# Cross-attention with layer norm: the last two tiles' probabilities transposed on TensorE, and a new order for the last ten tiles

## The chip, the cores and the metric

One NeuronCore of a Trainium2 chip. The metric is the device time of one execution in microseconds; the time before is the median of three runs.

## The reference

`x` has 4 batches of 2048 rows of 512, the context 4 batches of 77 rows of 512; there are 16 heads of 32, and everything is f32.

```python
qs = (q @ wq).reshape(Bq, Lq, H, HD).transpose(0, 2, 1, 3)
ks_ = (k @ wk).reshape(Bq, Lk, H, HD).transpose(0, 2, 1, 3)
vs = (v @ wv).reshape(Bq, Lk, H, HD).transpose(0, 2, 1, 3)
scores = jnp.einsum('bhqd,bhkd->bhqk', qs, ks_) / jnp.sqrt(jnp.float32(HD))
scores = jnp.where(mask[:, None, :, :], -jnp.inf, scores)
attn_w = jax.nn.softmax(scores, axis=-1)
attn = jnp.einsum('bhqk,bhkd->bhqd', attn_w, vs)
attn = attn.transpose(0, 2, 1, 3).reshape(Bq, Lq, H * HD)
out = attn @ wo + q
mu = jnp.mean(out, axis=-1, keepdims=True)
var = jnp.mean((out - mu) ** 2, axis=-1, keepdims=True)
return (out - mu) / jnp.sqrt(var + EPS) * gamma + beta
```

The queries `q` are `x`; keys and values both come from the context, and the mask says which of the 77 keys a batch leaves out.

## The kernel before

The 8192 rows are worked through in 64 tiles of 128 rows (tile 0 to 63); two tiles make a block, four a group, 16 a batch. The keys and values of all batches are made once at the start and stay in SBUF. To keep f32 accuracy at the speed of TensorE's rounded f32 type (`F32R`), the large products take three matmuls: both operands are split into a rounded high part and the remainder, and high×high, high×low and low×high are added in PSUM.

A tile goes through these steps. The letter is the one that names the step in the written order.

- `Q`, `q` (`q_visit`, `q_evac`): a quarter of a group's queries on TensorE (12 matmuls), copied from PSUM by VectorE. `i`, `j` split the transposed input `xT` into `xth` and `xtl` on ScalarE and GpSimd.
- `S` (`scores`): the scores of the 16 heads in four PSUM banks, plain f32, small matmuls packed into parts of the array.
- `T` (`maxima`, four quarters per tile) on VectorE: adds the mask and finds each head's maximum, into `pbuf`. `e` (`exps`, four quarters) on ScalarE: exponential and sum.
- `r` and `n` on VectorE and GpSimd: reciprocal of the sums, and the probabilities times it. `h` and `m` are the same for half of the heads.
- `t` (`transp`) on VectorE: transposes `pbuf` in 32×32 squares into `B`. `P` (`regroup_part`): 12 DMAs per block, from SBUF to SBUF, gather the squares into `PT`, where the keys lie along the partitions, 96 of them (77, and 19 again, so that even and odd heads can share one layout). For the last block each tile has 12 DMAs of its own, `U` (`regroup_tile`).
- `V` (`av`, per block) or `W` (`av_tile`, per tile): probabilities times values on TensorE. `a`, `b` split the result into `AH` on ScalarE and `AL` on VectorE; `c` and `d` do it for one tile.
- `O` (`o_proj`): the output projection, 12 matmuls of 512 columns. `+` (`residual`): VectorE adds the row of `x` that `x` (`load_x`) loaded. For four tiles `X` (`resid`) adds it in PSUM instead, as a plain f32 matmul with the identity.
- The layer norm, on whichever engine the order names: `s` statistics on VectorE, or `I` and `J` mean and squares on ScalarE; `u` the reciprocal root on GpSimd; then `y` (centre, times gamma) and `z` (times the root, plus beta) on VectorE, or `k` (ScalarE) or `p` (GpSimd) with `f` (gamma and beta on GpSimd), or `K` (times the root, on ScalarE) and `G` (plus beta, on GpSimd). `M` copies gamma or beta into a PSUM bank. `w` stores on SyncE's queue.

Tiles 0 to 53 run in a loop with a fixed order. For the last ten tiles the order is a written list, `ORDER`: words like `T63.2` (step, tile, part) or `P30.4g` (with the engine whose queue issues the DMA: `s`, `a`, `g`). Every engine carries out its own instructions in the order in which the words stand, and waits in it where data or a buffer is missing. PSUM's eight banks are given out in turn by `bank()`, except those that `M` has taken.

Of the kernel before, what the change touches and what calls it, by code (L numbers as in the profile page):

```python
# [8 lines left out]
F32 = mybir.dt.float32  # L9
# [8 lines left out]
P = 128  # L18
# [20 lines left out]
CUT = 27  # L39

# [5 lines left out]
i31 S54 Q59 T54.2 e54.2 x50 k46 T54.1 j31 T54.0 x56 q58 T54.3 S55 x59 O49 q59 e54.1 e54.3 T55.1 T55.0 T55.2 t53  # L46
e54.0 e55.1 S56 r54 P26.7g Q61 x61 x58 k47 T55.3 e55.3 V25 P26.2s T56.3 n54 x51 T56.0 e55.0 +49 x57 P26.3s e55.2 f46
P26.4s T56.1 T56.2 q61 S57 a25.0 t54 r55 n55 T57.0 e56.1 P26.9s T57.1 b25.0 s49 P26.1g w46 Q63 T57.2 P26.0s O48
a25.1 b25.1 S58 e56.0 t55 e56.3 P27.8s e56.2 Q62 T57.3 q63 P26.6g e57.2 Q60 P26.10g e57.0 f47 r56 P26.8s e57.1 T58.2
P26.11s T58.3 T58.1 T58.0 P26.5g P27.1s x52 x60 +48 P27.7g e57.3 P27.3s e58.3 n56 P27.0g e58.1 S59 P27.10g q62 t56  # L50
r57 s48 V26 q60 e58.2 T59.0 a26.1 T59.1 S60 e58.0 P27.2g T59.2 P27.11g O51 n57 t57 e59.2 T59.3 P27.5g a26.0 e59.3
O50 T60.1 x53 P27.9s T60.3 r58 T60.0 +51 b26.1 e59.0 b26.0 P27.4s e59.1 T60.2 P27.6s e60.0 P28.6s P28.2g S61 P28.10s
u48 e60.2 P28.3s n58 t58 P28.1s +50 r59 T61.2 V27 T61.1 x54 P28.11s P28.7s T61.0 T61.3 O53 P28.4s e60.3 P28.8g n59
t59 w47 S62 P28.0g a27.1 b27.1 O52 P29.6g e60.1 a27.0 T62.2 s51 b27.0 e61.0 e61.3 P28.5s e61.1 P29.8g P28.9s T62.1
P29.2g r60 n60 O54 +53 T62.0 s50 S63 e61.2 T62.3 t60 e62.1 e62.3 P29.0g +52 u50 u51 x55 r61 T63.2 e62.0 O55 n61
T63.0 P29.3s e62.2 +55 T63.1 P29.9s P29.7s t61 V28 +54 P29.4s P29.10s P29.5s T63.3 p50 a28.0 b28.0 a28.1 P29.11s M0
r62 P29.1s x62 P30.3s e63.3 f50 s55 P30.2s P30.1s V29 P30.10s P30.7g n62 b28.1 y55 P30.9s a29.0 v51 a29.1 P30.5s X59
P30.6s b29.0 P30.4s s54 O56 I52 P30.11s P30.8s t62 e63.0 e63.1 y48 e63.2 P30.0g U62.7s u54 b29.1 k51 u55 h63.0 w50
O57 m63.0 +56 h63.1 I56 U62.9s U62.3s O59 U62.11s U62.6s U62.0g s53 y52 U62.8s U62.2s V30 m63.1 J52 M1 x63 a30.0 s59
t63 y59 U62.5a +57 U62.4a U63.9a J56 O58 y49 U63.3s U63.8s U63.10s z55 U62.1g b30.0 u49 a30.1 f51 X62 U63.2a U63.5s  # L60
b30.1 X61 U63.6s O60 u56 U63.1a y54 U63.0s z48 O61 w55 u53 U63.11s u52 z49 z54 U63.4a I57 y53 +58 U62.10a u59 p56
J57 I61 W62 z53 U63.7s f56 w51 +60 s58 u57 W63 z52 w48 u58 s60 z59 u60 X63 y60 w49 c62 w56 J61 y57 d62 w52 c63 d63
w59 w54 w53 z60 u61 O62 z57 w60 O63 p58 f58 y61 I62 z61 J62 w57 y62 u62 w58 s63 z62 w61 y63 u63 z63 w62 w63
# [4 lines left out]
def xattn_layernorm(  # L68
# [53 lines left out]
    ident = ident[:, :P]  # L122
    mhalf, mneg, gates = small[:, 0:2], small[:, 2:4], small[:, 4:5]
    pbuf = [const.tile([P, NP, PW], F32, name=f"pbuf{i}") for i in range(NPB)]
# [18 lines left out]

    def keys_of(h):
        return slice(TAIL_K, NK2) if h % 2 == 0 else slice(0, NK)
# [3 lines left out]
    od, pos, mvs, rns, vd, ris, ends = {}, {}, {}, {}, {}, {}, {}  # L149
# [160 lines left out]
    def maxima(t, lo, hi):  # L310
        pb = pbuf[t % NPB]
        mb = bat[t // TPB][0]
        nm = nmax[t]
        for h in HEADS[lo:hi]:
            g, j = divmod(h, GH)
            nc.vector.tensor_tensor_reduce(  # L316
                pb[:, h // 2, (h % 2) * NK : (h % 2 + 1) * NK],
                scs[t][j][:, g * NK : (g + 1) * NK],
                mb[:, t % TPB, keys_of(h)],
                -1.0,  # L320
                3.0e38,
                ALU.add,
                ALU.min,
                accum_out=nm[:, h : h + 1],
            )
# [22 lines left out]
    def half_view(ap, r):  # L348
        return ap.rearrange("p (g r a) -> p g r a", r=2, a=2)[:, :, r]
# [6 lines left out]
    def normalise_half(t, r):  # L356
        pv = pbuf[t % NPB].rearrange("p (g r) w -> p g r w", r=2)[:, :, r, : 2 * NK]
        pv = pv.rearrange("p g (a k) -> p g a k", a=2)
        rv = half_view(ris[t], r)[:, :, :, None]
        nc.gpsimd.tensor_tensor(pv, pv, rv.to_broadcast((P, NG, 2, NK)), ALU.mult)  # L360

    def transp(t):
# [3 lines left out]
        if b < NBLK - 1:  # L366
            bt = bts[b].rearrange("p c (q t r) -> p c q t r", q=NP, t=2)[:, :, :, tt, :]
        else:
            bt = bts[b].rearrange("p c (t q r) -> p c q t r", q=NP, t=2)[:, :, :, tt, :]
# [5 lines left out]
    def regroup_part(b, n, queue, cols=slice(0, 2 * NP * 32)):  # L375
# [12 lines left out]
    def regroup_tile(t, n, queue):  # L388
        tt = t % 2
        regroup_part(t // 2, n, queue, slice(tt * NP * 32, (tt + 1) * NP * 32))  # L390


    def av(b):
# [3 lines left out]
        for g in range(NG):  # L397
            for j in range(GH):
# [4 lines left out]
                    pt[:NK2, :, h % 2, h // 2].rearrange("p i t r -> p t i r"),  # L403
# [4 lines left out]
    def av_tile(t):  # L408
        b, tt = divmod(t, 2)
        pt = pts[b].rearrange("p i a (t q r) -> p i a t q r", q=NP, t=2)  # L410
        pas[b, tt] = bank(f"pa_{b}_{tt}")
        for g in range(NG):
            for j in range(GH):
# [3 lines left out]
                    vsb[:, t // TPB, HD * h : HD * (h + 1)],  # L417
                    pt[:NK2, :, h % 2, tt, h // 2],
# [19 lines left out]
    def load_x(t):  # L438
# [6 lines left out]
        else:  # L445
            if t // 2 not in ends:
                ends[t // 2] = sb.tile([P, 2, GRP], F32, tag="xtf", name=f"o_end_{t}")
            od[t] = ends[t // 2][:, t % 2]
        nc.sync.dma_start(od[t], x[t * P : (t + 1) * P, :])

    def resid(t):
        pos[t] = bank(f"po_{t}")
        nc.tensor.matmul(pos[t], ident, od[t], start=True, stop=False)

    def o_proj(t):
# [9 lines left out]
        for n, (_, c, a, w) in enumerate(prods):  # L465
            nc.tensor.matmul(pos[t], a[:, c, rs], w[:, c, :], start=(first and n == 0), stop=(n == 11))  # L466
# [36 lines left out]
    def moments_one(t):  # L503
        st = sb.tile([P, 6], F32, tag="st", bufs=3, name=f"st_{t}")
        nc.vector.bn_stats(st, pos.get(t, od[t]))
        mvs[t, 1] = sb.tile([P, 4], F32, tag="mvt", bufs=64 - LATE, name=f"mvt_{t}")
        nc.vector.bn_aggr(mvs[t, 1][:, :2], st)

    def act_mean(t):
        if "junk" not in ends:  # L510
            ends["junk"] = sb.tile([P, NG, GRP], F32, tag="q", name="junk")
        mvs[t, 1] = sb.tile([P, 4], F32, tag="mvt", bufs=64 - LATE, name=f"mvt_{t}")
        nc.scalar.activation(
            ends["junk"][:, t % NG], pos.get(t, od[t]), AF.Identity, scale=1.0 / D, accum_out=mvs[t, 1][:, 0:1]
        )

    def act_squares(t):
        mv = mvs[t, 1]
        nc.scalar.activation(
            ends["junk"][:, t % NG], pos.get(t, od[t]), AF.Square, bias=mv[:, 0:1], scale=-1.0, accum_out=mv[:, 1:2]  # L520
# [32 lines left out]
    def centre(t):  # L553
        row = gam if t in pos else rows.get(0, gam)
        nc.vector.scalar_tensor_tensor(od[t], pos.pop(t, od[t]), mvs[t, 1][:, 0:1], row, ALU.subtract, ALU.mult)

# [295 lines left out]
```

## Time and profile before

| | us |
|---|---|
| median of three runs | 515.69 (515.43 to 515.73) |
| profiled execution, its own time | 516.79 |
| span of the profiled execution, first to last instruction | 515.0 |
| TensorE (PE) busy | 503.8 |
| VectorE (DVE) busy | 473.5 |
| ScalarE (ACT) busy | 470.3 |
| GpSimd (POOL) busy | 418.7 |

All terms below are made against the span of 515.0 us. A row of the timeline gives the start, the duration, the engine, the line of the kernel, the operation, what it writes and reads, the shapes and a count; in brackets stands the idle time of the engine before it and what ended that. A matmul's duration reaches into the next one's, so the cost of a run of matmuls is the distance between starts. SPq, ACTq and the like are the queues that issue DMAs.

### The profile page before, as it was taken

Reading aid. Unit: us, or ns where it says so; the run is one execution under the profiler, and the core shown is the slowest. Engines: PE = TensorE matmul, PEld = TensorE weight load, DVE = VectorE, ACT = ScalarE, POOL = GpSimd, SP = SyncE. Lnnn points to the kernel's source line nnn. Section 1 sums busy time; section 2 is a strip of 40 time slices with the busy share of each in tenths; the row PEclk is TensorE's granted clock in tenths of the full one; section 3 lists DMA queues with packets and bytes.
Section 4 is the critical chain, followed back from the end, with each engine's and each line's share of the span. In section 5 each row is a group of like instructions: output and inputs, shape, how many; then the busy total and the mean of one; then the engine's idle time right before and its main releaser. Section 6 shows DMA issues by size and latency. Waiting matters only on the chain.

```text
span 515.0 us, 20430 instructions
## 1 busy us (share of the span) xinstructions
PE 503.8 (98%) x6836; PEld 385.2 (75%) x6836; DVE 473.5 (92%) x2572; ACT 470.3 (91%) x2240; POOL 418.7 (81%) x376
## 2 busy tenths in 40 slices
PE   8999999999999999999999999999999999999994
PEld 6987777777877777787777777777777777777672
DVE  6798999899998888999999899889999989899996
ACT  6798999999899999999899999999899999999841
POOL 1659349988898988888889989889889988857996
PEclk9999999999999999999999999999999999999999
DMA  8946876878887878787878888777868778786665
GB/s 319 396 138 162 208 187 178 227 200 206 228 214 208 231 211 229 215 205 202 212 206 224 234 218 214 203 198 223 227 193 229 200 207 233 183 222 176 175 210 209
DMA packets 58937, 110.24 MB, mean 214 GB/s; under 512 B 9393, under 2 KB 11313, under 8 KB 58833
## 3 DMA queue, kind: packets, MB, share of 16 engines
q1 hardware_dynamic: 56000, 103.36, 73.3%
q0 software_dynamic: 2128, 4.85, 3.5%
q8 instruction: 55, 0.90, 0.8%
q10 hardware_dynamic: 704, 0.72, 0.5%
q14 instruction: 50, 0.40, 0.2%
HBM read 41.79 MB, written 16.78 MB: 114 GB/s over the span
## 4 chain that ended last, share of the span: by engine, by line
PE 83%; DMA 5%; POOL 4%; DVE 4%; SPq 2%; issue 1%; ACT 0%; DVEq 0%; POOLq 0%
PE pq L170 30%; PE po L466 29%; PE sc L302 10%; PE pa L400 10%; DMA PT<-B 4%; SPq L382 2%; PE pv L236 2%; DVE B L370 1%; PE pk L196 1%; PE pq L599 1%; POOL mvt L532 1%; DVE pbuf L316 1%; POOL o_end L545 1%; DMA xtf<-xT 1%; POOL o_end L496 1%
## 5 line engine op out<-in xcount | busy, mean ns | idle before, releaser
L330 ACT ACTIVATE pbuf<-pbuf,nm 128x77 f32<-128x77 f32 x1024 | 352.5, 352 | 16.2 <-DVE nm L316 14.8
L330 ACT ACTIVATION_READ_ACCUMULATOR pbuf<-pbuf,nm 128x1 f32 x1024 | 196.9, 192 | 0.0
L316 DVE CUSTOM_DVE_ANT_0 pbuf<-sc,mb 128x77 f32<-128x77 f32 x1024 | 170.7, 230 | 23.3 <-PE sc L302 23.2
L346 POOL TENSOR_TENSOR pbuf<-pbuf,ri 128x1232 f32<-128x1232 f32 x63 | 142.2, 2258 | 22.9 <-DVE ri L341 16.1
L170 PE MATMUL pq<-xth,wqh 128*128 128x512 f32 (+1 forms) x256 | 98.8, 386 | 0.0
L170 PE MATMUL pq<-xtl,wqh 128*128 128x512 f32 (+1 forms) x256 | 97.9, 382 | 0.0
L170 PE MATMUL pq<-xth,wql 128*128 128x512 f32 (+1 forms) x256 | 97.9, 382 | 0.0
L370 DVE STREAM_TRANSPOSE B<-pbuf 128x1280 f32<-128x1280 f32 x64 | 95.5, 1493 | 2.2 <-DMA PT<-B 1.8
L466 PE MATMUL po<-woh,AH 128*128 128x512 f32 x232 | 96.9, 418 | 0.0
L466 PE MATMUL po<-wol,AH 128*128 128x512 f32 x232 | 90.6, 391 | 0.0
L466 PE MATMUL po<-woh,AL 128*128 128x512 f32 x232 | 88.9, 391 | 0.0
L316 DVE DVE_READ_ACCUMULATOR2_ANT nm<- 128x1 f32 x1024 | 84.0, 82 | 0.0
L496 POOL TENSOR_TENSOR o<-o,gam 128x512 f32<-128x512 f32 x50 | 65.6, 1311 | 14.1 <-ACT o L492 14.0
L302 PEld LDWEIGHTS sc<-kct,q 32*64 32x64 f32 x4096 | 51.6, 130 | 24.4 <-issue 23.0
L497 POOL TENSOR_TENSOR o<-o,bet 128x512 f32<-128x512 f32 x50 | 64.5, 1289 | 3.9
L163 POOL TENSOR_TENSOR xtl<-xtf,xth 128x1024 fp32r<-128x1024 f32 x28 | 67.1, 2397 | 0.0
L302 PE MATMUL sc<-kct,q 32*64 32x77 f32 x4096 | 62.1, 237 | 0.7 <-DVE nm L316 0.3
L400 PE MATMUL pa<-PT,vsb 96*32 96x256 f32 x960 | 58.0, 382 | 1.5 <-DMA PT<-B 1.2
L170 PEld LDWEIGHTS pq<-xth,wqh 128*128 128x128 f32 x256 | 48.1, 188 | 9.8
L170 PEld LDWEIGHTS pq<-xth,wql 128*128 128x128 f32 x256 | 48.1, 188 | 9.4
L170 PEld LDWEIGHTS pq<-xtl,wqh 128*128 128x128 f32 x256 | 48.1, 188 | 9.1
L466 PEld LDWEIGHTS po<-woh,AH 128*128 128x128 f32 x232 | 43.5, 187 | 13.0 <-issue 0.7
(141 smaller groups left out, 689.4 us busy)
## 6 DMA issues: line engine op xcount, KB each, us to landing
PT<-B SPq DMA_DIRECT2D x352, 128.0 KB, 2.9
xtf<-xT SPq DMA_DIRECT2D x28, 512.0 KB, 5.3
o<-x SPq DMA_DIRECT2D x56, 256.0 KB, 5.6
out<-o SPq DMA_DIRECT2D x56, 256.0 KB, 2.6
PT<-B POOLq DMA_DIRECT2D x20, 128.0 KB, 4.0
o_end<-x SPq DMA_DIRECT2D x8, 256.0 KB
out<-o_end SPq DMA_DIRECT2D x8, 256.0 KB, 2.1
xtf<-xT SPq DMA_DIRECT2D x4, 256.0 KB
```

The source lines that it names most:

```text
L163: nc.gpsimd.tensor_tensor(l, fx.pop((g, c)), h.bitcast(F32), ALU.subtract)
L170: nc.tensor.matmul(pq, w[:, c, m * P : (m + 1) * P], r[:, c, rs], start=(n == 0), stop=(n == 11))
L236: nc.tensor.matmul(pv, ctx_s[c][i][:, r, :], v[c], start=(n == 0), stop=(n == 11))
L302: nc.tensor.matmul(sc[j][half : half + P // 2, g * NK : (g + 1) * NK], qs[q, g, r0 : r0 + P // 2], kct[q, g, t // TPB, keys_of(j)], start= ...
L316: nc.vector.tensor_tensor_reduce(pb[:, h // 2, (h % 2) * NK : (h % 2 + 1) * NK], scs[t][j][:, g * NK : (g + 1) * NK], mb[:, t % TPB, keys_ ...
L330: nc.scalar.activation(pb[:, h // 2, (h % 2) * NK : (h % 2 + 1) * NK], pb[:, h // 2, (h % 2) * NK : (h % 2 + 1) * NK], AF.Exp, bias=nmax[t ...
L346: nc.gpsimd.tensor_tensor(pv, pv, rv.to_broadcast((P, NP, 2, NK)), ALU.mult)
L370: nc.vector.transpose(bt.rearrange("p c q r -> p q c r"), pbuf[t % NPB].rearrange("p q (c r) -> p q c r", c=5),)
L400: nc.tensor.matmul(pas[b, g // 2][HD * j : HD * (j + 1), (g % 2) * BLK : (g % 2 + 1) * BLK], vsb[:, 2 * b // TPB, HD * h : HD * (h + 1)], ...
L466: nc.tensor.matmul(pos[t], a[:, c, rs], w[:, c, :], start=(first and n == 0), stop=(n == 11))
L496: nc.gpsimd.tensor_tensor(o, o, gam, ALU.mult)
L497: nc.gpsimd.tensor_tensor(o, o, bet, ALU.add)
```

## The change

For tiles 62 and 63 the squares (`t`) and the regrouping DMAs (`U`) go. Instead `R` (`flip`) transposes the probabilities of four heads at a time on TensorE, 77×128 each, into a PSUM bank, and `E` (`flip_evac`) copies the bank to `PT` on ScalarE or VectorE; `W` then reads 77 rows. Since even and odd heads had their keys in different orders, odd heads need the values of the last batch in the other order: two small DMAs (`Y`, `turn_values`) make that copy. The heads get new places in `pbuf` (`slot`), so that the half that is normalised first is contiguous.

Of the four residuals on TensorE, those of 59, 61 and 62 go back to VectorE; that of 63 is made by eight matmuls from the split transposed input that is still in SBUF, without loading `x` again. The last tile's projection runs over the left 256 columns, then the right 256; its statistics are taken per half, and its last multiply and its store go by halves on two queues. The list for tiles 54 to 63 is new throughout, with other choices of engine for the layer norms. Some of its ends, before and after:

```
- ... V28 V29 X59 O56 O57 O59 V30 O58 X62 X61 O60 O61 W62 W63 X63 O62 O63     (TensorE's words from V28 on)
+ ... V28 S62 O54 O56 O57 S63 V29 R62.3 R62.0 R62.1 R62.2 O59 O58 W62 V30 R63.0 R63.1 O62 R63.2 O61 R63.3 O60 W63 X63 O63
- ... u59 p56 f56 u57 u58 u60 u61 p58 f58 u62 u63                            (GpSimd's last words)
+ ... u57 u51 u54 f49 u56 v54 m63.0 v52 u53 m63.1 f54 u55 u58 u62 f52 G58 u59 u61 u60 G61 u63
- ... a30.1 U63.2a U63.1a U63.4a I57 U62.10a J57 I61 c62 J61 c63 I62 J62      (ScalarE's last words)
+ ... e63.2 M1 c62 a30.1 a30.0 M0 k54 I58 E63.0a J58 k52 I62 J62 E63.1a K58 E63.2a E63.3a I61 J61 c63 I60 J60 K61 z63
- ... z57 y61 z61 y62 s63 z62 y63 z63                                        (VectorE's last words)
+ ... z62 +60 y61 z55 d63 z59 y60 z60 s63 y63 z63
```

```diff
+    def slot(h):
+        g, j = divmod(h, GH)
+        return 2 * (NG * (j // 2) + g) + j % 2
...
+    def flip(t, i):
+        pr = flips[t, i] = bank(f"pr_{t}_{i}")
+        for k in range(GH):
+            q, a = divmod(GH * i + k, 2)
+            nc.tensor.transpose(pr[:NK, k * P : (k + 1) * P], pbuf[t % NPB][:, q, a * NK : (a + 1) * NK], ident)
+
+    def flipped(t):
+        b, tt = divmod(t, 2)
...
+        return pts[b].rearrange("p i a (x r) -> p (i a x) r", r=P)[:NK, tt * H : (tt + 1) * H]
+
+    def flip_evac(t, i, copy):
+        copy(flipped(t)[:, GH * i : GH * (i + 1)], flips.pop((t, i))[:NK].rearrange("p (h r) -> p h r", r=P))
...
     def av_tile(t):
...
-                    vsb[:, t // TPB, HD * h : HD * (h + 1)],
-                    pt[:NK2, :, h % 2, tt, h // 2],
+                    (spare(NG - 1)[:NK] if h % 2 else vsb[:NK, NB - 1])[:, HD * h : HD * (h + 1)],
+                    pt[:, slot(h)],
...
     def resid(t):
         pos[t] = bank(f"po_{t}")
-        nc.tensor.matmul(pos[t], ident, od[t], start=True, stop=False)
+        if t < NT - 4:
+            nc.tensor.matmul(pos[t], ident, od[t], start=True, stop=False)
+            return
+        place(t)
+        for c in range(NC_D):
+            for n, part in enumerate(gx[t // 4]):
+                rows_t = part[:, c, t % 4 * P : (t % 4 + 1) * P]
+                nc.tensor.matmul(pos[t][:, c * P : (c + 1) * P], rows_t, unit, start=(c == 0 and n == 0), stop=False)
...
-        for n, (_, c, a, w) in enumerate(prods):
-            nc.tensor.matmul(pos[t], a[:, c, rs], w[:, c, :], start=(first and n == 0), stop=(n == 11))
+        halves = [slice(0, D)] if t < NT - 1 else HALVES
+        for cols in halves:
+            for n, (_, c, a, w) in enumerate(prods):
+                go = first and n == 0 and cols.start == 0
+                done = n == 11 and cols.stop == D
+                nc.tensor.matmul(pos[t][:, cols], a[:, c, rs], w[:, c, cols], start=go, stop=done)
...
+            for n, cols in enumerate(HALVES):
+                nc.vector.bn_stats(st[:, n], pos.get(t, od[t])[:, cols])
...
+    def turn_values():
+        v = spare(NG - 1)
+        nc.sync.dma_start(v[:TAIL_K], vsb[NK:, NB - 1])
+        nc.sync.dma_start(v[TAIL_K:NK], vsb[: NK - TAIL_K, NB - 1])
...
+    def finish_last(t):
+        for cols, queue in zip(HALVES, (nc.sync, nc.scalar)):
+            o = od[t][:, cols]
+            nc.vector.scalar_tensor_tensor(o, o, mvs[t, 1][:, 2:3], rows.get(1, bet)[:, cols], ALU.mult, ALU.add)
+            queue.dma_start(out[t * P : (t + 1) * P, cols], o)
```

More of the change, by code (lines that the diff above doesn't have):

```diff
@@ L55 @@
[L55 to L63, printed above, removed]
+S54 T54.0 x56 i31 q58 T54.3 T54.2 O48 T54.1 j31 S55 T55.2 e54.0 t53 +48 Q59 x58 T55.1 e54.3 O49 q59 x51 T55.0 P26.0s
@@ L64 @@
++61 y59 E63.2a E63.3a z62 +60 I61 y61 W63 z55 w53 G58 J61 w49 w54 u59 w52 c63 I60 u61 d63 J60 K61 u60 z59 w62 y60
+z60 w58 w59 X63 O63 w55 s63 G61 w60 y63 w61 u63 z63 w63
 """
@@ L776, in do @@
             scale_one(k)
+        elif op == "z" and k == NT - 1:
+            finish_last(k)
+        elif op == "w" and k == NT - 1:
+            od.pop(k)
         elif op in tile_ops:
```

104 lines of the change are left out of this document (58 added, 46 removed).

## The prediction

> **What bounds the kernel now.** I read the page first (busy shares, chain that ended last), then TensorE's timeline, then the last 12 us of all engines, then the busy time by stretches.
>
> ```profile
> span 515.0 us, 20430 instructions
> PE 503.8 (98%) x6836; PEld 385.2 (75%) x6836; DVE 473.5 (92%) x2572; ACT 470.3 (91%) x2240; POOL 418.7 (81%) x376
> PE 83%; DMA 5%; POOL 4%; DVE 4%; SPq 2%; issue 1%; ACT 0%; DVEq 0%; POOLq 0%
> ```
>
> TensorE carries 83% of the chain. Busy matmuls overlap, so 98% alone proves little; what proves it is the distance between starts. Here are the first score matmul of tile 54 (where the hand-written order begins), the only four places after it where TensorE's timeline marks idle time, and its last matmuls.
>
> ```profile
> 420.54 0.48 PE L302 MATMUL sc<-kct,q 32*64 32x77 f32 x26
> ...
> 448.15 1.93 PE L400 MATMUL pa<-PT,vsb 96*32 96x256 f32 x32 [0.29 <-DMA o<-x]
> ...
> 451.06 0.89 PE L302 MATMUL sc<-kct,q 32*64 32x77 f32 x58 [0.32 <-DVE nm L316]
> ...
> 458.81 1.93 PE L400 MATMUL pa<-PT,vsb 96*32 96x256 f32 x32 [0.29 <-DMA PT<-B]
> ...
> 503.94 1.20 PE L466 MATMUL sc<-woh,AL 128*128 128x512 f32 x4 [0.27 <-DVE AL L435]
> ...
> 506.79 1.07 PE L466 MATMUL sc<-woh,AL 128*128 128x512 f32 x4
> ```
>
> From 420.54 to 507.86 (506.79 + 1.07) TensorE works 87.3 us and idles 1.2 (0.29 + 0.32 + 0.29 + 0.27). So up to 507.9 the time is the sum of TensorE's work. The rest of the span, 7.15 us, is the tail of tile 63:
>
> ```profile
> 507.65 1.26 POOL L497 TENSOR_TENSOR o_end<-o_end,bet 128x512 f32<-128x512 f32 x1
> 507.90 0.70 DVE L505 BATCH_NORM_STATS2 st<-sc 128x6 f32<-128x512 f32 x1
> 508.63 0.18 DVE L507 BATCH_NORM_AGGREGATE mvt<-st 128x2 f32<-128x6 f32 x1
> 508.89 0.26 POOL L529 TENSOR_SCALAR mvt<-mvt,nz 128x1 f32<-128x1 f32 x1
> 508.94 3.52 SPq L500 DMA_DIRECT2D out<-o_end  x4
> 509.24 0.56 POOL L532 TENSOR_TENSOR mvt<-mvt,small 128x1 f32<-128x1 f32 x1
> 509.77 0.19 POOL L531 TENSOR_TENSOR mvt<-mvt,nz 128x1 f32<-128x1 f32 x1
> 509.83 0.75 DVE L558 SCALAR_TENSOR_TENSOR o_end<-o_end,mvt,sc 128x512 f32<-128x512 f32 x1 [1.02 <-POOL mvt L532]
> 510.04 0.55 POOL L532 TENSOR_TENSOR mvt<-mvt,small 128x1 f32<-128x1 f32 x1
> 510.50 0.74 DVE L555 SCALAR_TENSOR_TENSOR o_end<-sc,mvt,gam 128x512 f32<-128x512 f32 x1
> 511.35 0.75 DVE L558 SCALAR_TENSOR_TENSOR o_end<-o_end,mvt,sc 128x512 f32<-128x512 f32 x1
> ```
>
> The statistics of tile 63 are ready at 508.81, but GpSimd is still adding beta to tile 58 (until 508.91), then does the root of tile 62, and comes to that of 63 only at 509.77. VectorE idles 1.02 us for tile 62. The last multiply ends at 512.10; 2.9 us later (store and close) the span ends.
>
> **The transposing path is long, but TensorE does not wait for it.**
>
> ```profile
> 470.15 0.95 PE L302 MATMUL sc<-kct,q 32*64 32x77 f32 x64
> 485.61 1.23 POOL L360 TENSOR_TENSOR pbuf<-pbuf,ri 128x616 f32<-128x616 f32 x1 [0.75 <-DVE ri L354]
> 487.40 1.24 POOL L360 TENSOR_TENSOR pbuf<-pbuf,ri 128x616 f32<-128x616 f32 x1
> 488.67 1.51 DVE L370 STREAM_TRANSPOSE B<-pbuf 128x1280 f32<-128x1280 f32 x1 [0.31 <-POOL pbuf L360]
> 498.82 1.95 PE L415 MATMUL pa<-PT,vsb 96*32 96x128 f32 x64
> 500.70 1.13 PE L453 MATMUL sc<-o_end,ident 128*128 128x512 f32 x2
> ```
>
> Scores of tile 63 start at 470.15, its probabilities are normalised at 488.64, and 10.2 us of transpose and regrouping DMAs lie between that and the attention-times-value matmuls at 498.82. TensorE shows no idle time at 498.82: other tiles' projections cover it. Cutting those 10.2 us therefore gives nothing directly. It lets the order put other work earlier, and it costs TensorE the transposes. Gain and loss are to be sought in TensorE's sum and in the tail.
>
> **The change part by part.** TensorE first; the prices:
>
> ```profile
> 481.27 0.39 PE L466 MATMUL po<-woh,AH 128*128 128x512 f32 x1
> ...
> 483.99 0.39 PE L466 MATMUL sc<-woh,AH 128*128 128x512 f32 x1
> ...
> 491.52 1.88 PE L453 MATMUL sc<-o_end,ident 128*128 128x512 f32 x4
> 492.83 0.79 PE L466 MATMUL po<-woh,AH 128*128 128x512 f32 x1
> 493.46 0.40 PE L466 MATMUL po<-wol,AH 128*128 128x512 f32 x1
> ```
>
> ```profile
> 5.09 5.99 PE pq L599 x48
> ```
>
> A projection of 12 matmuls with 512 columns takes 2.72 us (481.27 to 483.99), 0.227 each. The opening's 48 matmuls with 256 columns take 5.99 us, 0.125 each. Two residual matmuls X62 and X61 (plain f32) last from 491.52 to 493.46 less one projection matmul: 1.71 us, 0.86 each.
>
> 1. X59, X61 and X62 leave TensorE for VectorE's add: 3 × 0.86 = **−2.6 us**.
> 2. X63 becomes eight matmuls of 128 columns (high and low part of the transposed input against the identity). The line through 512 and 256 columns gives 0.074 us at 128; a quarter of the f32 residual gives 0.215. Eight are 0.6 to 1.7 us, against 0.86 before. I take 1.0, as the operands are of the split type that the 0.125 row ran: **+0.1** (−0.3 to +0.8).
> 3. 32 transposes (two tiles × 16 heads), each a load of 77 columns and a pass of 128. No transpose on TensorE is in this trace. Below: 0.065, under the line's 0.074. Above: 0.215, if plain f32 takes several passes as the residual does. I take 0.09, near the line, with something for weight loads that do not hide: **+2.9** (+2.1 to +6.9).
> 4. O63 in halves: 24 × 0.125 = 3.0 instead of 2.72: **+0.3**.
> 5. Attention times value of tiles 62 and 63 keeps its 16 heads of 128 columns per tile (1.88 us for both, 498.82 to 500.70); 77 instead of 96 rows change no column count, and the new slots of the heads in the buffer change addresses alone: 0.
> 6. Idle time: the first three of the four waits belong to places that the new order rearranges. I let 0.8 of the 1.2 us go (0 to 1.2): **−0.8**.
>
> The sum is −0.1, so the last matmul ends at about 507.8 again.
>
> The tail. Without f58 and p58 GpSimd ends with u60, the beta of 61, then u63; u62 is long past, since O62 now precedes O61 and O60. Half of O63's columns get their statistics while TensorE does the other half. After the last matmul: 0.04 + about 0.42 for 256 columns (between 0.35, half of 0.70, and 0.70) + 0.03 + 0.18 = 0.67; then 0.08 + 0.81 for u63 (509.77 to 510.58, with its gap) = 1.56, under which y63 (0.74) hides; two half multiplies end at about 2.05 and 2.45, each storing on a queue of its own; then the same 2.9 us. Together 5.35 instead of 7.15: **−1.8** (−2.1 if the smaller stores land sooner, 0 if GpSimd is late).
>
> The other engines:
>
> ```profile
> core 0: us, PE busy (x) PEld busy (x) DVE busy (x) ACT busy (x) POOL busy (x), PEclk, DMA share, GB/s
> 490.00:500.00 10.00, 10.00 (x80) 7.51 (x82) 9.96 (x18) 3.55 (x10) 9.44 (x14) 1.00 0.77 239
> 500.00:510.00 10.00, 7.59 (x55) 5.23 (x46) 8.81 (x16) 3.17 (x8) 9.39 (x15) 1.00 0.52 198
> ```
>
> ```profile
> L431 ACT CAST AH<-pa 128x512 fp32r<-128x512 f32 x12 | 6.9, 586 | 0.3 <-PE pa L415 0.3
> L187 DVE COPY q<-pq 128x512 f32<-128x512 f32 x6 | 4.1, 679 | 0.0
> ```
>
> Eight copies of transposed probabilities are added: six on ScalarE (6 × 0.59 = 3.5 us by the PSUM cast's row) and two on VectorE (2 × 0.68 = 1.4). VectorE loses two transposes (2 × 1.51 = 3.0) and gains three adds. ScalarE is the engine with room: 6.7 of the 20 us from 490 to 510 are busy. The copies are free as long as that room lasts; without it each costs its 0.59. The 24 regrouping DMAs and the load x63 leave the queues; two small copies of value rows (Y0) come in ahead of P30's parts on SyncE's queue. V30 reads P30 behind some 10 us of TensorE work, so two issues more are hidden.
>
> Waits are added. TensorE's in-order queue has R63.0 to R63.3 among projections, so a late m63.0 or m63.1 on GpSimd holds O62, O61 and O60 too. On ScalarE, E63.2a and E63.3a stand behind K58, which waits for u58 on GpSimd, and E63.1a behind J62, which needs O62; W63 and O63 wait for all of them. From S63 to W63 TensorE now has S63 itself (0.95), W62 (0.94, half of the 1.88), V29 and V30 (two tiles each, so 1.88 each by the same row), five projections (O59, O58, O62, O61, O60: 13.6) and the 32 transposes (2.9): 22 us. The path from scores to normalised probabilities was 18.5 us (470.15 to 488.64), and the last transposes with their copy add about 1.3. So the cover exceeds the need by some 2 us: enough, but thin.
>
> −0.1 and −1.8 make −1.9: a span of 513.1. The profiled execution took 516.79 us, its span 515.0, the median of the runs is 515.69; taking the difference over, 515.69 − 1.9 = **513.8**.
>
> [...] The granted clock is 1.00 in both rows above, where TensorE runs ordinary matmuls without a pause, and a matmul's duration (0.39) overlaps the next, which starts 0.227 later. [...]
>
> **The rivals.**
> - *Transposes at the price of a plain f32 matmul or of an unoverlapped one.* 0.215 (a quarter of the residual), and nearly the same if none overlaps the next (0.39 − 0.227 + 0.074 = 0.24): 4.0 us more than I took, **517.8**, slower. It decides from 1.9/32 = 0.06 us above my 0.09, so from 0.15 each. For it: the residual is plain f32 and does take 0.86. Against: a transpose moves data and need not multiply in passes. [...] Chance 0.16.
> - *The last softmax arrives late.* The 2 us of cover are used up because copies, statistics and GpSimd's roots interlock ahead of W63; TensorE then waits at R63 or W63. With the path 5.5 us longer, 3.5 are paid: **517.3**, slower; it decides from a path 4 us longer (2 of cover and the 1.9 of gain). For it: VectorE and GpSimd are 9 to 10 tenths busy there. Against: ScalarE's room. Chance 0.14.
> - *The tail does not shrink.* The beta of 61 holds GpSimd when u63 is due, as that of 58 did; only the half statistics and half multiplies remain (about 0.6 us): **515.0**. Chance 0.08.
> - *All goes well:* transposes at 0.065 and no idle time: −0.8 − 0.4, and the input matmuls at 0.6: **512.2**. Chance 0.10.
>
> **How the numbers follow.** My forecast has 0.52. The range 511.8 to 517.8 takes in the bounds of the transposes and of the waits; outside lie mainly longer stalls and the 0.275 us price. About 0.2% (1 us) is what a measurement of this kernel can tell from no change. Faster by more: 0.48 of my case, the 0.10 and 0.03 of the third rival, 0.61. Same: 0.04, 0.05 of the third, 0.04 of the first two: 0.13. Slower: 0.26.
>
> **What would show it.** Right: in the profile after, the 16 transposes of a tile take about 1.5 us from first to last start; TensorE's idle marks after tile 54 stay near a microsecond and its last matmul ends near 508; from there to the end are about 5.4 us, with GpSimd idle when tile 63's statistics land; ScalarE's idle time in the last 20 us is gone. Wrong: transposes 0.15 us or more apart, a lower granted clock around them, idle marks at the transposes or at W63 that name ScalarE or GpSimd, or a GpSimd addition that overlaps the last statistics.

## The result, and the profile after

The changed kernel takes 517.83 us (median of 20 executions, 515.81 to 522.39), the kernel before 515.94 in the same runs (515.43 to 518.09). The ratio is 1.0032, with a 95% interval of 1.0016 to 1.0048: slower by 0.3%, where 0.4% faster was forecast. The profiled execution took 518.36 us, its span is 516.5. A few executions of either kernel run several us over its median, with waits in the loop; the profiled ones of e2 and e4 below (spans of 522.6 and 521.5) are such, and no lengths are read from them.

The page of the changed kernel, busy times and chain:

```profile
span 516.5 us, 20502 instructions
PE 506.0 (98%) x6880; PEld 390.9 (76%) x6880; DVE 473.1 (92%) x2573; ACT 474.7 (92%) x2249; POOL 426.0 (82%) x382
PE 87%; DVE 5%; ACT 4%; DMA 1%; POOL 1%; issue 1%; SPq 0%; DVEq 0%; POOLq 0%
```

GpSimd has 7.3 us more work than before (426.0 against 418.7), ScalarE 4.4 more. TensorE's timeline from tile 54 on, with every idle time that it marks:

```profile
421.55 0.95 PE L309 MATMUL sc<-kct,q 32*64 32x77 f32 x64
...
457.41 1.93 PE L411 MATMUL pa<-PT,vsb 96*32 96x256 f32 x32 [0.21 <-issue]
...
482.06 1.93 PE L411 MATMUL pa<-PT,vsb 96*32 96x256 f32 x32 [1.47 <-DMA PT<-B]
483.93 1.97 PE L392 MATMUL pr<-ident,pbuf 128*77 128x128 f32 x16
485.65 0.48 PE L491 MATMUL po<-woh,AH 128*128 128x512 f32 x1
...
505.69 0.33 PE L474 MATMUL po<-ident,xth 128*128 128x128 f32 x1
...
507.53 0.38 PE L491 MATMUL po<-woh,AH 128*128 128x256 f32 x1 [0.73 <-ACT AH L442]
...
510.02 0.64 PE L491 MATMUL po<-woh,AL 128*128 128x256 f32 x4
```

And the tail, all engines:

```profile
509.98 0.75 DVE L602 SCALAR_TENSOR_TENSOR o_end<-o_end,mvt,row 128x512 f32<-128x512 f32 x1 [0.25 <-POOL mvt L570]
510.70 0.76 DVE L535 BATCH_NORM_STATS2 small<-po 128x6 f32<-128x256 f32 x2
511.50 0.21 DVE L537 BATCH_NORM_AGGREGATE mvt<-small 128x2 f32<-128x12 f32 x1
511.79 0.19 POOL L569 TENSOR_TENSOR mvt<-mvt,nz 128x1 f32<-128x1 f32 x1 [0.60 <-DVE mvt L537]
512.05 0.55 POOL L570 TENSOR_TENSOR mvt<-mvt,small 128x1 f32<-128x1 f32 x1
512.64 0.87 DVE L598 SCALAR_TENSOR_TENSOR o_end<-o_end,mvt,row 128x256 f32<-128x256 f32 x2
513.14 0.33 SPq L599 DMA_DIRECT2D out<-o_end  x1
513.54 0.36 ACTq L599 DMA_DIRECT2D out<-o_end  x1
```

From these rows and those of before, the span falls into three parts:

| part of the span, us | before | after | difference | forecast |
|---|---|---|---|---|
| start to the scores of tile 54 | 420.54 | 421.55 | +1.0 | 0 |
| scores of 54 to the end of the last matmul ("the stretch") | 87.3 | 89.1 | +1.8 | -0.1 |
| from there to the end (the tail) | 7.15 | 5.9 | -1.3 | -1.8 |

TensorE's work in the first part is the same in both kernels. What differs most there is the opening. In the chain of waits the 48 opening matmuls, 5.99 us long before, now read:

```profile
5.20 7.96 PE pq L643 x48
```

The timeline shows where it changes its pace (four matmuls to a row):

```profile
0.93 3.60 PE L612 MATMUL pw<-ident 128*128 128x512 bf16 x8 [0.93 <-POOL ident L605]
5.20 1.19 PE L643 MATMUL pq<-xth,wqh 128*128 128x256 f32 x4 [0.68 <-ACT xth L144]
...
8.75 1.05 PE L643 MATMUL pq<-xtl,wqh 128*128 128x256 f32 x4
9.61 0.67 PE L643 MATMUL pq<-xth,wql 128*128 128x256 f32 x4
10.12 0.64 PE L643 MATMUL pq<-xth,wqh 128*128 128x256 f32 x4
```

Up to 9.6 us four matmuls take 0.85, from then on 0.48 (10.12 to 10.60, the next row). In the kernel before they take 0.48 from 5.64 us on. The granted clock shows nothing of it:

```profile
5.00:10.00 5.00, 4.80 (x24) 4.83 (x24) 4.36 (x10) 3.71 (x9) 0.00 (x0) 1.00 1.00 368
```

The columns are those of the busy times in the prediction. From 5 to 10 us TensorE is busy 4.80 us with 24 matmuls at a clock of 1.00; before it did 41 in that time, also at 1.00.

The first scores stand at 22.99 us instead of 20.91. Half of these 2.1 us comes back by tile 54, in the main because the kernel before met a wait of 0.88 us for a regrouping DMA at 127.0 us that the changed one did not meet.

### The profile page after: what moved, and what is told of

Same layout as the page of the kernel before. It is cut to its first block, busy times and chain, and to the rows that moved or that the text cites. A ratio compares the mean times of both kernels' runs of the same rounds, so it can differ in the third digit from the quotient of the medians.

```text
span 516.5 us, 20502 instructions
## 1 busy us (share of the span) xinstructions
PE 506.0 (98%) x6880; PEld 390.9 (76%) x6880; DVE 473.1 (92%) x2573; ACT 474.7 (92%) x2249; POOL 426.0 (82%) x382
## 4 chain that ended last, share of the span: by engine, by line
PE 87%; DVE 5%; ACT 4%; DMA 1%; POOL 1%; issue 1%; SPq 0%; DVEq 0%; POOLq 0%
PE pq L177 32%; PE po L491 30%; PE sc L309 10%; PE pa L411 10%; ACT pbuf L339 3%; PE pv L243 2%; PE pq L643 2%; PE pk L203 1%; DVE pbuf L324 1%; DVE B L370 1%; DMA xtf<-xT 1%; DMA PT<-B 1%; DVE AL L446 0%; DVE o_end L593 0%; SPq L382 0%
## 5 line engine op out<-in xcount | busy, mean ns | idle before, releaser
L491 PE MATMUL po<-woh,AH 128*128 128x512 f32 (+1 forms) x252 | 103.3, 411 | 0.7 <-ACT AH L442 0.7
L491 PE MATMUL po<-wol,AH 128*128 128x512 f32 (+1 forms) x252 | 97.3, 387 | 0.0
L491 PE MATMUL po<-woh,AL 128*128 128x512 f32 (+1 forms) x252 | 93.2, 387 | 0.5 <-issue 0.5
L370 DVE STREAM_TRANSPOSE B<-pbuf 128x1280 f32<-128x1280 f32 x62 | 92.3, 1492 | 0.0
L521 POOL TENSOR_TENSOR o<-o,gam 128x512 f32<-128x512 f32 x53 | 69.4, 1310 | 14.2 <-ACT o L517 14.1
L522 POOL TENSOR_TENSOR o<-o,bet 128x512 f32<-128x512 f32 x53 | 68.7, 1295 | 4.2
L411 PE MATMUL pa<-PT,vsb 96*32 96x256 f32 x992 | 60.1, 382 | 1.8 <-DMA PT<-B 1.5
L491 PEld LDWEIGHTS po<-woh,AH 128*128 128x128 f32 x252 | 47.3, 188 | 13.9 <-ACT AH L442 0.9
```

Source lines behind the costliest of these rows:

```text
L370: nc.vector.transpose(bt.rearrange("p c q r -> p q c r"), pbuf[t % NPB].rearrange("p q (c r) -> p q c r", c=5),)
L411: nc.tensor.matmul(pas[b, g // 2][HD * j : HD * (j + 1), (g % 2) * BLK : (g % 2 + 1) * BLK], vsb[:, 2 * b // TPB, HD * h : HD * (h + 1)], ...
L491: nc.tensor.matmul(pos[t][:, cols], a[:, c, rs], w[:, c, cols], start=go, stop=done)
L521: nc.gpsimd.tensor_tensor(o, o, gam, ALU.mult)
L522: nc.gpsimd.tensor_tensor(o, o, bet, ALU.add)
```

## The experiments

Each run was timed in five rounds beside the kernel before on the same chip. For the end of the program I read one number from each trace: scores of tile 54 to the end of the span. It does not hold the opening. Before: 94.5, after: 95.0. Where the end of the program is the same, the number agrees within 0.2 us (before, e3 and e15; after, e1 and e16; e9 and e12). The part ahead of it does not: it ranges from 418.6 to 421.6 us over the profiles, and with ten warm-ups the kernel before (e15) and a version of the changed one (e13) both have 418.55.

| run | median, us | before there | ratio (95%) | stretch | tail | scores of 54 to the end |
|---|---|---|---|---|---|---|
| e1 after, 10 warm-ups | 516.54 | 515.86 | 1.0022 (1.0002-1.0042) | 89.1 | 5.9 | 95.0 |
| e2 before, 10 warm-ups | 515.54 | 515.86 | 1.0001 (0.9981-1.0021) | | | |
| e3 before, 2 warm-ups | 516.89 | 515.86 | 1.0028 (0.9996-1.0060) | 87.5 | 7.2 | 94.6 |
| e4 P29 by SyncE | 517.27 | 515.86 | 1.0025 (0.9996-1.0053) | | | |
| e5 m63.0 early | 517.77 | 516.05 | 1.0015 (0.9995-1.0036) | 89.1 | 5.8 | 94.9 |
| e6 J61 before y61 | 516.75 | 516.05 | 0.9999 (0.9981-1.0018) | 88.2 | 5.9 | 94.1 |
| e7 before, halves alone | 518.59 | 516.05 | 1.0032 (1.0009-1.0054) | 87.5 | 8.0 | 95.4 |
| e8 e5 + e6, statistics apart, 10 | 516.69 | 516.05 | 1.0021 (1.0001-1.0042) | 88.4 | 6.5 | 94.8 |
| e9 m63.0, m63.1 early + e6 | 517.22 | 515.36 | 1.0016 (0.9991-1.0040) | 88.3 | 6.3 | 94.6 |
| e10 after, O63 whole | 517.06 | 515.36 | 1.0034 (1.0005-1.0063) | 88.9 | 6.1 | 95.0 |
| e11 e9, transposes twice | 517.08 | 515.36 | 1.0040 (1.0019-1.0061) | 89.9 | 5.8 | 95.7 |
| e12 e9, 10 warm-ups | 515.35 | 515.36 | 0.9993 (0.9979-1.0007) | 88.3 | 6.3 | 94.6 |
| e13 e12, end reordered | 516.17 | 516.26 | 0.9991 (0.9973-1.0009) | 86.7 | 8.0 | 94.6 |
| e14 e13, two banks | 516.14 | 516.26 | 0.9983 (0.9960-1.0006) | 86.6 | 7.6 | 94.3 |
| e15 before, 10 warm-ups | 515.88 | 516.26 | 0.9987 (0.9972-1.0002) | 87.4 | 7.2 | 94.6 |
| e16 after, 10 warm-ups | 517.08 | 516.26 | 1.0014 (0.9988-1.0040) | 89.2 | 5.9 | 95.1 |
| e17 e13, tile 52 on VectorE | 515.27 | 515.49 | 0.9998 (0.9975-1.0020) | 86.6 | 7.2 | 93.8 |
| e18 e17, two banks | 515.08 | 515.49 | 0.9985 (0.9967-1.0002) | 86.6 | 7.1 | 93.8 |

**The opening.**

```diff
-WARM = 8
+WARM = 10   # e1 (after), e2 (before); e3 (before): 2
```

> The changed kernel with 10 warm-up matmuls on TensorE instead of 8, so that they reach to about 5.2 us, where the opening's first real matmul starts. Theory A (the opening's slow stretch is TensorE's own pace: in the changed kernel's profile its first 20 matmuls of 256 columns stand 0.21 us apart, the others 0.12, and the pace rises only after a stretch without a gap): the 48 opening matmuls take 6.0 to 7.3 us instead of 8.0, the median falls from 517.8 by 0.7 to 1.9, to 515.9 to 517.1, and the times spread less. Theory B (the loads or the casts set the opening's pace): 8.0 us again, median 517.8 as before. Theory C (the pace is chance of the moment, whatever stands ahead): the same two groups of times, about 516.2 and 517.9, in about the same shares.

> The kernel before with 10 warm-up matmuls instead of 8. Its profile shows the opening at full pace (48 matmuls in 5.99 us). Theory A: nothing left to gain in most executions, median 515.5 to 516.0, the runs above 516.2 become rarer. Theory B: 515.9. Theory C: 515.9 with the same spread. Read together with the changed kernel with 10: their difference is what the rest of the change is worth; theory A expects the changed one faster by 0.1 to 0.9 us, as its fastest runs have a span of 514.4 against 515.0.

> The kernel before with 2 warm-up matmuls instead of 8. Theory A: TensorE starts its real work cold in every execution; 16 to 32 of the opening matmuls stand 0.21 us apart, the opening takes 7.5 to 9.0 us instead of 6.0 and the median rises by 1.5 to 3 us, to 517.4 to 518.9. Theory B: no change, 515.9, as the loads arrive as before. Theory C: the share of slow executions stays as it was, 515.9.

With ten warm-ups the changed kernel's 48 matmuls take 5.98 us, and its span is 514.7 instead of 516.5. With two, the kernel before shows the changed kernel's slow opening: 7.39 us, the slow pace lasting to 8.3; its median rose by 1.0 us, less than theory A's 1.5. So the kernel before can have the slow pace too. The loads do not set it, since they are no sooner with ten (the load ahead of the first cast takes 3.81 us in e1, 3.70 in the changed kernel). The clearest pair came later, when the kernel of e9 was run with ten (e12) beside itself with eight on one chip. The chain of e9:

```profile
5.44 8.00 PE pq L643 x48
```

and of e12:

```profile
5.25 5.98 PE pq L643 x48
```

> The kernel of the run with both normalisations early, with ten warm-up matmuls instead of eight. Theory A (the opening's slow pace lasts longer where TensorE has a gap between warm-up and first matmul): first score matmul at 20.9 to 21.6 us, last matmul near 506.5, tail 5.9, span near 512.4, time near 514.3, 0.3% under before. Theory B (the pace of the opening is a matter of chance that ten warm-ups don't change): first score matmul anywhere from 20.9 to 23.2 us, and a median no better than that of the run with eight.

With eight warm-ups ten of twelve executions took 516.7 to 517.8 and two 515.1 to 515.3. With ten, all twelve took 515.1 to 515.8. The forecast of 514.3 was too low (the end shortened less than e9's theory wanted), but eight or ten warm-ups shift this kernel's median by 1.9 us. The profiles say the same of the opening alone: with ten, the 48 matmuls take 5.8 to 6.0 us in e1, e8 and e12 to e18; with eight, 7.9 to 8.2 in the changed kernel, e6, e9, e10 and e11, and 6.0 in e5, the kernel before and e7.

> The kernel before with ten warm-up matmuls, to compare with the next run on one chip. Theory A (the gap ahead of the first real matmul makes the opening slow in some executions): nearly all executions within 0.8 us of the lowest, median 515.0 to 515.4. Theory C (chance whatever stands ahead): as many 1.5 to 2 us above the lowest as with eight.

> The changed kernel with ten warm-up matmuls. Theory A (apart from the opening the change costs +1.8 us in the stretch and gives 1.3 in the tail): 0.4 to 0.6 us above the run of the kernel before with ten warm-ups. Rival (the opening hid no more than noise, the change costs all of the 1.9 us between the medians): 1.5 us or more above it.

The opening is not all that spreads the times: nine of e15's twelve executions lie more than 0.8 us above its lowest, against theory A, and e13 with ten ran from 515.1 to 517.2. With ten in both, 1.2 us lie between the medians (e16 less e15), and 1.0 in the first pair (e1 less e2), against 1.9 with eight. That is between theory A and its rival, and the rounds' intervals are as wide as the question. The end accounts for 0.4 to 0.5 (95.1 less 94.6). In e16's profile 1.2 us more went into one wait in the loop at 265.8 us, for which the trace names no releaser; such waits stand elsewhere or nowhere in the other profiles. What is left beyond these is open. Open too is why the changed kernel should meet the slow opening oftener than the one before.

**The wait for P29, and the last softmax.**

```diff
-... e62.3 +54 O56 P29.5g t61 P29.6g e62.2
+... P29.5s P29.6s e62.3 +54 O56 t61 e62.2
```

> The changed kernel with the parts P29.5 and P29.6 issued from SyncE's queue right behind P29.1 instead of from GpSimd's behind n61. In the profile V29 waited 1.47 us for the last part of P29, which GpSimd issued at 475.1 and which landed 6.5 us later. Theory A (that wait costs the time): the idle mark at V29 is gone, TensorE's last matmul ends 1.2 to 1.5 us earlier counted from the scores of tile 54, median 516.4. Theory B (the last softmax binds, the rival of the prediction): the mark at V29 goes, but m63.0 on GpSimd is no earlier, so TensorE waits for it at R63.0 by 1.1 to 1.5 us and ends within 0.4 us of where it did; median 517.5.

The wait at V29 fell to 0.2 us, and 1.56 us appeared at R63.0, named after GpSimd's `pbuf`. e1 shows the same, since there the DMAs happened to land early:

```profile
477.82 0.95 PE L309 MATMUL sc<-kct,q 32*64 32x77 f32 x64
479.09 1.93 PE L411 MATMUL pa<-PT,vsb 96*32 96x256 f32 x32 [0.31 <-DVE o_end L494]
...
492.67 0.66 PE L392 MATMUL pr<-ident,pbuf 128*77 128x128 f32 x4 [1.51 <-POOL pbuf L363]
```

The first row is S63. So the last softmax is late by itself; the wait for P29 only runs beside it. GpSimd's rows of e1 say why:

```profile
486.71 1.30 POOL L521 TENSOR_TENSOR o<-o,gam 128x512 f32<-128x512 f32 x1
488.09 1.61 POOL L522 TENSOR_TENSOR o<-o,bet 128x512 f32<-128x512 f32 x1
489.69 0.69 POOL L567 TENSOR_SCALAR mvt<-mvt,nz 128x1 f32<-128x1 f32 x1
490.46 0.55 POOL L570 TENSOR_TENSOR mvt<-mvt,small 128x1 f32<-128x1 f32 x1
490.99 0.19 POOL L574 TENSOR_TENSOR mvt<-mvt 128x1 f32<-128x1 f32 x1
491.25 0.19 POOL L575 TENSOR_TENSOR mvt<-mvt,small 128x1 f32<-128x1 f32 x1
491.40 1.22 POOL L363 TENSOR_TENSOR pbuf<-pbuf,ri 128x616 f32<-128x616 f32 x1
```

The normalisation m63.0 (L363) stands behind f49, u56 and v54, although its reciprocal was there at 487.6. Next run: m63.0 ahead of these three.

> Theory A: the last softmax comes late because its first normalisation (m63.0) stands on GpSimd behind f49, u56 and v54, although its reciprocal is there 3 to 4 us earlier; the wait for tile 58/59's regrouping at V29 only ran beside it. With both taken away (m63.0 ahead of u56, v54 and f49; the last two transfers of group 29 issued by SyncE) the first transposes of tile 63 (R63.0) wait under 0.2 us instead of 1.5, and the stretch from the scores of tile 54 to the last matmul is 87.6 us instead of 89.1. Theory B: VectorE and ScalarE have nothing earlier either; the wait comes back at R63.1, R63.2 or W63, and the stretch stays at 88.8 or more.

```profile
495.77 0.66 PE L392 MATMUL pa<-ident,pbuf 128*77 128x128 f32 x4 [1.49 <-POOL pbuf L363]
```

R63.0 waited no more, and R63.2 waited 1.49 us for m63.1, which f49 now held up. The stretch stayed at 89.1: theory B, by the same mechanism one step on.

**J61.** In the changed kernel ScalarE evicts tile 63's values (c63, L442) behind J61 (L557), and J61 stands behind y61 in the order:

```profile
506.19 0.72 ACT L557 ACTIVATE spare<-o_end,mvt 128x512 f32<-128x512 f32 x1 [1.84 <-DVE o_end L593]
506.82 0.19 ACT L557 ACTIVATION_READ_ACCUMULATOR spare<-o_end,mvt 128x1 f32 x1
506.91 0.56 ACT L442 CAST AH<-po 128x512 fp32r<-128x512 f32 x1
```

```diff
-... I61 y61 W63 z55 w53 G58 J61 w49 ...
+... I61 J61 y61 W63 z55 w53 G58 w49 ...
```

> Only the order of two words is changed: J61 stands ahead of y61, so that ScalarE no longer waits for VectorE before it evicts tile 63's values (c63). Theory A: O63's wait falls from 0.73 us to 0.1 or less, stretch 88.4 us instead of 89.1. Theory B: c63 is held by its own matmuls (W63) or by another engine, the wait stays at 0.5 us or more and the stretch at 89.0.

O63's wait is gone, the stretch is 88.2, and the end comes 0.9 us sooner after tile 54 (94.1): theory A, and more than the whole difference to the kernel before in that part (0.5).

> The changed kernel with the two edits above together, the first half's statistics ahead of z60 on VectorE, and ten warm-up matmuls instead of eight. Theory A (the new order's waits cost the time, not the transposes): stretch 89.1 - 1.5 - 0.7 = 86.9 us, tail 5.9 - 0.35 = 5.5 us, first score matmul between 21 and 22 us, span near 512.9 and time near 514.7, which is 0.2% under before. Theory B (the transposes and what they add on the other engines cost the time): the waits move on, stretch 88.5 us or more, time 516 or more.

> Both normalisations of tile 63 (m63.0 and m63.1) ahead of v54, v52, u53 and f49 on GpSimd, group 29's last two transfers on SyncE, and J61 ahead of y61. Theory A (GpSimd's queue in front of the last softmax is what holds TensorE): no wait over 0.3 us is left between the scores of tile 54 and the last matmul; the stretch is 86.6 to 86.9 us, less than the 87.3 of the kernel before. Theory B (VectorE or ScalarE is late as well): the wait of 1.5 us moves on a third time, to R63.3, W63 or O63, and the stretch is 88.2 or more.

Theory A failed in both. In e8 R63.2 waits 1.46 us, as in e5. In e9 theory B held: no wait is marked at R63, and TensorE reaches R63.0 1.8 us sooner after tile 54 than in e6, yet W63, X63 and O63 take 1.7 us longer (6.7 from the start of W63 to the last matmul's end, 5.0 in e6):

```profile
505.60 0.38 PE L491 MATMUL po<-woh,AH 128*128 128x256 f32 x1 [0.27 <-ACT AH L442]
507.17 0.74 PE L491 MATMUL po<-woh,AL 128*128 128x256 f32 x4 [0.36 <-DVE AL L446]
```

because on ScalarE K58 (L586) waits for GpSimd ahead of the copies E63.2 and E63.3 (L401):

```profile
501.93 0.72 ACT L586 ACTIVATE o_end<-o_end,mvt 128x512 f32<-128x512 f32 x1 [2.79 <-POOL mvt L570]
502.56 1.05 ACT L401 COPY PT<-pa 77x512 f32<-77x512 f32 x2
```

The additions that left the place ahead of m63 (f49 and what follows) now hold u58, on which K58 waits.

**The price of a transpose.** e11 is e9 with each transpose issued twice.

> The kernel of the run with both normalisations early, with each of the 32 transposes issued twice into the same place. Theory A (with the waits gone TensorE is the bound, and a transpose costs its spacing of 0.103 to 0.108 us): the stretch grows by 3.0 to 3.4 us. Theory B (transposes run in time that TensorE would wait anyway): it grows by less than 1.5 us.

```profile
482.09 3.72 PE L393 MATMUL pr<-ident,pbuf 128*77 128x128 f32 x32
```

TensorE reaches W63 3.35 us later than in e9 (84.9 us after tile 54's scores against 81.55): 0.105 each. But the last matmul comes only 1.7 us later, and the end 1.2. The theories split: the price is A's, and two thirds of it vanish before the end, because TensorE alone does not set the end there.

**Who sets the end.**

```diff
-... R63.3 O60 K58 +61 y59 E63.2a E63.3a z62 ...
+... R63.3 O60 E63.2a E63.3a K58 +61 y59 z62 ...
-... I61 J61 y61 W63 z55 w53 G58 w49 w54 u59 w52 c63 I60 u61 d63 ...
+... I61 J61 W63 c63 d63 y61 z55 w53 G58 w49 w54 u59 w52 I60 u61 ...
```

(and f54 behind u62)

> The run with everything early and ten warm-ups, and in the last 12 us two more moves: on ScalarE the last two copies of tile 63 (E63.2, E63.3) ahead of K58, which waits for GpSimd; on VectorE d63 ahead of y61 and z55; on GpSimd f54 behind u55, u58 and u62. Theory A (what took back the 1.6 us won at R63 is K58's wait for GpSimd ahead of the copies, and d63 behind two steps of other tiles): W63 takes 1.0 us instead of 1.6, O63 3.1 instead of 3.7, the stretch is 86.6 to 87.0 us, span near 511.5, time near 513.6. Theory B (ScalarE, VectorE and GpSimd have too much to do in the last 15 us in any order): a wait of 1 us or more is left in W63 to O63, stretch 88.0 or more, time 515 or more.

The stretch is 86.7, as theory A said, with no mark of idle time over 0.21 us left. The end did not move at all: the tail grew to 8.0. VectorE's rows after the last matmul (505.20):

```profile
505.00 0.75 DVE L602 SCALAR_TENSOR_TENSOR o_end<-o_end,mvt,row 128x512 f32<-128x512 f32 x1 [1.06 <-POOL mvt L570]
505.66 0.74 DVE L593 SCALAR_TENSOR_TENSOR o_end<-o_end,mvt,pr 128x512 f32<-128x512 f32 x1
506.77 0.75 DVE L602 SCALAR_TENSOR_TENSOR o_end<-o_end,mvt,row 128x512 f32<-128x512 f32 x1 [0.37 <-POOL mvt L570]
507.44 0.76 DVE L535 BATCH_NORM_STATS2 small<-po 128x6 f32<-128x256 f32 x2
```

Tile 63's statistics wait 2.2 us behind steps of other tiles that wait for GpSimd, and GpSimd works without a pause:

```profile
489.00:508.00 19.00, 16.20 (x136) 13.29 (x124) 15.80 (x27) 12.68 (x28) 17.93 (x29) 1.00 0.53 194
```

17.93 of 19 us busy, the rest gaps of some 0.1 us between instructions. So I took some 3 us of work from it (and 0.8 from ScalarE):

```diff
-v52 ... k52 ... f52
+y52 ... z52        # VectorE
```

> The run with the reordered end, with tile 52's last steps (v52, k52, f52: 3.0 us on GpSimd, 0.8 on ScalarE) done by VectorE instead (y52, z52: 1.5 us, in the gaps of 1.0 and 1.1 us that it had at 501 and 504 us). Theory A (in the last 20 us GpSimd is the wall: it worked without a pause from 488.8 to 508.0 us there, and TensorE's earlier end only lengthened the tail): tail 5.9 to 6.3 us instead of 8.0, first score matmul of tile 54 to the end 92.7 to 93.2 us instead of 94.6, time 1.5 us or more under the kernel before in the same state of the opening. Theory B (VectorE is as full, or the stores set the end): 94.2 us or more from the scores of tile 54 to the end.

The end came 0.8 us sooner (93.8), between the two theories; now VectorE has hardly a pause:

```profile
502.00:509.50 7.50, 3.29 (x28) 3.09 (x27) 7.15 (x13) 2.16 (x5) 3.69 (x8) 1.00 0.55 212
```

GpSimd held the end by some 0.8 us, and VectorE is full right behind it. By the median e17 cannot be told from the kernel before.

**The halves.**

> The kernel before with one part of the change alone: tile 63's projection in two column halves, statistics of each half, last step and store in halves. Theory A: the tail is 5.9 us instead of 7.15 and the last matmul ends 0.25 us later, so the span is 1.0 us shorter. Theory B: VectorE is in another tile's work when the first half is there and the store's fixed part sets the end: tail 6.7 us or more, the span within 0.3 us of before.

> The changed kernel with tile 63's projection, statistics, last step and store whole again. Theory A (the statistics of the first half wait for the last matmul of the second, so halves only add instructions): the last matmul 0.25 us earlier, the tail 5.7 to 5.9 us, the span not longer than with halves. Theory B (the halves shorten the tail): tail 6.5 us or more.

e7 put the store of tile 62 behind the first half's store (513.20 us, 3.7 before the end), so its longer tail says little about halves. e10, the undoing in the changed kernel: the last matmul 0.2 earlier, the tail 0.2 longer, the end the same. The halves give this kernel nothing. e8 shows why best, where VectorE had come to the first half's statistics in time:

```profile
508.19 0.43 DVE L534 BATCH_NORM_STATS2 small<-po 128x6 f32<-128x256 f32 x1 [0.51 <-PE po L491]
```

VectorE waits 0.51 us, until the last matmul of both halves is done (508.15), though the first half's are done by 506.72. Whether the common bank or the program's own wait does it, this run does not tell.

> The run with the reordered end, with tile 63's two column halves in two PSUM banks, the first half's statistics ahead of z60 on VectorE, and y63 in two halves. Theory A (with both halves in one bank the first half's statistics wait for the last matmul of the second): they now start about 1.5 us before the last matmul ends, and the tail is 0.35 us shorter than without. Theory B (something else holds VectorE): they start after the last matmul as before, tail the same or longer.

> The run before in this list with tile 63's halves in two PSUM banks and the first half's statistics ahead of z60. Theory A: with GpSimd out of the way the first half's statistics run under the last matmuls and the tail is 5.4 to 5.6 us. Theory B (z60 and y60 still stand on VectorE behind GpSimd's additions when the last matmul ends): tail within 0.2 us of the run without the two banks.

With a bank for each half the end came 0.4 us sooner in e14, nothing in e18. In both, VectorE was still at other tiles' steps when the last matmul ended, so whether the first half can run under the second was not seen. e18 is the best version that I have: 0.9985 of the kernel before, with an interval up to 1.0002, so not shown to be faster.

## Why the prediction was wrong

The forecast was a span 1.9 us shorter; the profile's is 1.5 longer. Of these 3.4 us, 1.0 lie ahead of tile 54, 1.9 in the stretch (+1.8 for -0.1) and 0.5 in the tail (-1.3 for -1.8).

**The work of TensorE was right.** Without the marked idle times the stretch is 86.7 us (89.1 less 0.21, 1.47 and 0.73) against 86.15 before (87.3 less 1.17): +0.55, forecast +0.7. The 32 transposes cost 3.3 us (the 16 of tile 62 stand 1.72 apart from first to next, 0.108 each) instead of 2.9; X63's eight matmuls 0.95, forecast 1.0; O63 3.13, forecast 3.0. The higher price of a transpose that the forecast's range leaves outside is shown by no run: this case's f32 transposes cost 0.105 to 0.108 us by spacing and by doubling, and one record's 0.27 us overlaps the next. The projection right behind the 16 keeps its spacing of 0.23 us (485.97 to 486.20), with a granted clock of 1.00 from 483.93 to 486.20, so no slower pace followed them.

**Step 6, the idle time, had the wrong sign.** It let 0.8 us go; 1.2 came on top (2.41 marked against 1.17). The old waits did go, but new ones came, and two make up most of the 2.41: 1.47 at V29, beside which the last softmax ran just as late (m63.0 ends at 494.47, R63.0 starts at 494.52), and 0.73 at O63, for J61's place behind y61, which no rival named. The first is the second rival, but not at its price and not by its working. The wait that the profile names (a DMA) was not the one that binds, as e4 and e1 show.

The step that failed is the cover. I summed what TensorE has to do between S63 and W63 (22 us) against a path read from the trace before (18.5), and found 2 us to spare. But the matmul that first needs tile 63's probabilities is R63.0, and TensorE's queue keeps its order (in the profile after, V30 starts at 492.40, R63.0 at 494.52, O62 at 495.37). Ahead of R63.0 stand S63, V29, the 16 transposes of tile 62, O59, O58, W62 and V30, which is 12.5 us by the prediction's own prices. Against that stands the first half's normalisation, which ended 16.7 us after the scores in the trace before (470.15 to 486.84). By these numbers a wait of some 4 us was due. In e1 R63.0 starts 14.85 us after S63 (477.82 to 492.67), 13.0 of work and 1.8 of waits. The path had become shorter; the work ahead of R63.0 was too little to cover it. Yet undoing this wait gained nothing by itself (94.9 in e5, 94.6 in e9, against 94.1 in e6), since the steps put behind m63 then held up later ones. Of the two waits only J61's was a plain loss.

**The first paragraph, "the time is the sum of TensorE's work", holds only while TensorE is late.** In the changed kernel the end still follows the last matmul: e6 brought both 0.9 us sooner. Further on it does not. With TensorE's marked waits gone (e13 against e12) the last matmul came 1.6 us sooner and the end did not move, and doubling the transposes (e11) moved the end by a third of their price. I priced the new row-wise work on ScalarE and VectorE and never summed GpSimd's, which has 7.3 us more; in e13 it has no pause from 489 to 508 us, and e17, with some 3 us of its work moved, ends 0.8 us sooner.

**The tail** shrank by 1.3 instead of 1.8. GpSimd is idle when tile 63's statistics land, as forecast. "Half of O63's columns get their statistics while TensorE does the other half" failed: they start at 510.70, after the last matmul (510.66). VectorE was at z60 until then (509.98 to 510.73), and e8 shows that they wait even where it is free. They are done 1.05 us after the last matmul instead of 0.67, which is most of the missing 0.5.

**The opening was no part of the forecast.** It gives +2.1 us, of which 1.0 remains at tile 54. By 94.5 against 95.0 the end of the changed program costs 0.5 us, less than a median of this kernel tells; e6 shows that the order of two words costs more. With ten warm-ups in both, the medians lie 1.0 and 1.2 apart, and what makes up the rest is not shown. That the change saves 1.9 us was wrong in either reading.

## What to carry to other kernels

When an engine's work is traded for another's at the end of a program, sum every engine's queue for the new order, not only the bound one's: a wait removed from TensorE came back three times, each time at the next word that stood behind GpSimd. Count the cover of a long path only up to the first instruction in the waiting engine's queue that needs the data. A wait that the profile names may run beside a longer one; take it away before counting it as gain. Before a difference of 0.3% is laid to a change, compare the parts of the two programs that are the same.

## What the hardware showed unexpectedly

The first matmuls ran at half pace (0.21 us for 256 columns instead of 0.12) until 9.6 us in the changed kernel's profile, and at full pace from 5.64 us in that of the kernel before, whose TensorE has the same work there, with a granted clock of 1.00 from 5 to 10 us in both. With two more warm-ups the kernel of e9 took 5.98 us for these 48 matmuls (e12) instead of 8.00. What sets the pace is not shown, and the granted clock of these profiles did not show the slow pace.

Two of block 29's regrouping DMAs, issued by GpSimd at 474.6 and 475.1 us, landed 4.9 and 6.5 us later; the median of GpSimd's is 4.6, of SyncE's 3.0. And a GpSimd step on 128x1 (L574, v54) ahead of m63.0 took 1.85 us in the changed kernel's profile (from 491.17), the same step of v52 0.19 (from 494.42); VectorE was at work beside both, and the cause is open.
